# A gated block with attention and a Hadamard feed-forward: gate and up as features by tokens, the norm from squares, a new order

## The chip, the cores and the metric

The kernel runs on one core of a Trainium2 chip. The metric is device time in microseconds, the median of several executions. TensorE is called PE here, its weight loads PEld, VectorE DVE, ScalarE ACT, GpSimd POOL, and the queue that issues most transfers SP.

## What is computed

Sixteen batches of 128 tokens and 512 features go through attention on a given context and then through a feed-forward whose activations are rotated by a Walsh-Hadamard transform and rounded to 8 bits, and whose weights are rounded to -1, 0 or 1.

```python
x = x + tanh(g_xattn[0]) * xattn(layernorm(x), ctx, ctx)      # 32 query heads, 8 key heads, width 16
x = x + tanh(g_ffn[0]) * ffn(layernorm(x), w_gate, w_up, w_down)

def h_bitlinear(x, w):
    return einsum('bsh,oh->bso', act_quant(fwht(x)), weight_quant(w))
def act_quant(x):      # per token
    scale = 127.0 / clip(max(abs(x), axis=-1), EPS)
    return clip(round(x * scale), -128, 127) / scale
def weight_quant(w):
    scale = clip(mean(abs(w)), EPS)
    return clip(round(w / scale), -1, 1) * scale
def ffn(h, w_gate, w_up, w_down):          # 512 -> 2048 -> 512
    gate, up = h_bitlinear(h, w_gate), h_bitlinear(h, w_up)
    return h_bitlinear(silu(gate) * up, w_down)
```

## The kernel before

The kernel is cut into small step functions, one for each batch `b` and part. A step may `yield`, and each mention of it in the text `ORDER` (line 23) runs it on to its next `yield`; a token such as `gate.9.1` stands for `gate(9, 1)`. The order of the tokens is the program order, and the class `InOrder` keeps every engine to it, so that all instructions have the line of that helper (249) in the profile. Each engine works strictly through its own list, and waits where an operand is not ready. There is no loop and no scheduler beside that text: it alone interleaves the batches.

A batch passes through these steps:

- Attention: `moments_q` (line 390; mean and variance on DVE, three small POOL operations), `normed` (ACT), `q_transposed`, `scores` (PE, with maxima `mx` on DVE out of PSUM), `split_max` (four small POOL operations), a transpose of the maxima, `weights` (PE tiles `sT`, exponentials `ex` on ACT), `summed` (PE tiles `av`), `residual` (line 522; PE transposes `tpo`, DVE `rden` and `ga`, POOL adds into `x`).
- Into the feed-forward: `moments_h` (line 635) and `in_norm` (line 638): a second layer norm, `hn` on ACT, then two butterfly stages on POOL (tiles `hn`, `hb`); `in_turned` and `in_hadamard` (PE, tile `z`); `in_scale` (line 672), the largest magnitude on DVE and from it the scale `ae`, its inverse `re` and, on POOL, the two factors `dq` with which gate and up are to be scaled back; `in_quant` (line 682), rounding on ACT into `qe`, a transposing transfer by SP into `qTe`, and a conversion.
- `gate` and `up` (lines 708 and 714), in two halves `m` of 1024 features each. `product` (line 696) holds the 128 tokens as the stationary operand and streams 512 columns of weights: the result has tokens on partitions. ACT makes Silu of the gate with the token's factor `dq` as its scale, into `sg`; DVE multiplies up by its factor and by `sg`, into `h`.
- `hidden_transposed` (line 723): four PE transposes (`tpf`) for each 512 features and a copy `hT`, as the Hadamard transform wants features on partitions. `hadamard`, `hadamard_l` and `hadamard_p` (PE, tile `y`, a 128-point transform; the last two take one butterfly stage with it) and a copy into `za` or `zb`; `butterfly` on DVE; `magnitudes` on ACT.
- `out_scale`, `out_quant` (line 816 on; DVE, then a transposing transfer into `qTf`), `out_down` (line 872; PE tile `yo`, then on DVE the last scaling and the addition of `x`, tile `res`, which SP writes out).

Weights are loaded, summed up (`mag`), averaged (`mean`), rounded (`whole`) and clipped while the first batches are in attention. `warm` are matmuls without use ahead of the first work, `table` loads an activation table (0: the one with exponentials, 1: with Silu); the build adds a load wherever an activation finds the wrong table. `copies[k]` (line 358) is ACT for `k` = 0 and DVE for 1; `k` is the last number of many tokens. PSUM has two pools: `ps_s`, two buffers of two banks, for scores, weights, gate and up, and `ps_x`, four of one bank, for the rest.

Of the kernel before, what the change touches and what calls it, by code (L numbers as in the profile page):

```python
# [23 lines left out]
load_kv0 load_aux warm.0.12 load_x1 load_g.1 fetch.2 moments_q.0 load_g.0 load_g.3 table.0.0  # L24
gates_in load_sel moments_q.0 normed.0 q_transposed.0 load_g.2 q_transposed.0 mag_g.1 scores.0.1
fetch.4 load_u.2 moments_q.1 moments_q.1 warm.1.6 scores.0.1 scores.0.1 normed.1 moments_q.2
scores.0.0 moments_q.2 load_u.3 q_transposed.1 scores.0.0 warm.2.8 q_transposed.1 values_in.1
mag_g.0 scores.0.0 values_in.0 moments_q.3 load_u.1 scores.1.1 mag_g.3 moments_q.3 warm.3.4
scores.1.1 load_u.0 warm.4.2 scores.1.1 split_max.0 max_transposed.0.1 normed.2 max_transposed.0.1
scores.1.0 sel_in mag_g.2 q_transposed.2 scores.1.0 scores.1.0 warm.5.6 mean_g q_transposed.2  # L30
normed.3 weights.0.1 mean_g whole_g.3 whole_g.1 warm.6.8 weights.0.1 weights.0.1 whole_g.0 load_d.0
load_d.3 weights.0.0 moments_q.5 moments_q.5 summed.0.1 mag_u.3.1 weights.0.0 load_d.2 weights.0.0
split_max.1 mag_u.2 scores.2.1 clipped_g.0 max_transposed.1 scores.2.1 summed.0.0.1 max_transposed.1
summed.0.1 residual.0.1 scores.2.1 whole_g.2.1 summed.0.0.1 weights.1.0 residual.0.1 moments_q.4
q_transposed.3.1 weights.1.0 residual.0.0 q_transposed.3.1 weights.1.0 residual.0.0 residual.0.0
mag_u.0 scores.2.0 moments_q.4 summed.1.0 residual.0.1 summed.1.0 scores.2.0 scores.2.0 mag_u.1
residual.1.0 split_max.2 weights.1.1 moments_h.0 clipped_g.3 residual.1.0 moments_h.0
max_transposed.2.1 weights.1.1 fetch.6 mean_u warm.7.8 max_transposed.2.1 mean_u weights.1.1
load_d.1 whole_u.1 in_norm.0 scores.3.1 normed.4 in_norm.0 scores.3.1 whole_u.0.1 q_transposed.4
summed.1.1 in_norm.0 scores.3.1 q_transposed.4 whole_u.3 residual.1.0 normed.5 scores.3.0  # L40
in_turned.0 scores.3.0 in_turned.0 values_in.3 whole_u.2.1 scores.3.0 in_hadamard.0 in_scale.0
split_max.3 weights.2.1 summed.1.1 clipped_u.3 residual.1.1 moments_q.6 moments_q.6 weights.2.1
weights.2.1 max_transposed.3.1 q_transposed.5.1 clipped_g.2 residual.1.1 in_quant.0 weights.2.0
in_quant.0 max_transposed.3.1 moments_q.7 residual.1.1 mag_d.0.1 weights.2.0 values_in.2 summed.2.1
weights.2.0 moments_h.1 moments_h.1 normed.6 weights.3.1 summed.2.1 q_transposed.5.1 clipped_u.1
residual.2.1 weights.3.1 clipped_u.2 q_transposed.6.1 summed.2.0 weights.3.1 residual.2.1 in_quant.0
clipped_g.1 weights.3.0 in_norm.1 mag_d.2.1 summed.2.0 in_norm.1 summed.3.1 fetch.8 weights.3.0
residual.2.0 weights.3.0 in_scale.0 gate.0.0 residual.2.0 residual.2.0 clipped_u.0 mag_d.1.1 up.0.0
table.1.1 gate.0.0 in_norm.1 summed.3.1 mag_d.3 gate.0.1 residual.2.1 q_transposed.6.1 moments_q.7
up.0.0 in_turned.1.1 hidden_transposed.0.1 in_turned.1.1 mean_d up.0.1 moments_h.2  # L50
hidden_transposed.0.1 mean_d moments_h.2 in_hadamard.1 gate.0.1 up.0.1 values_in.4 summed.3.0
values_in.5 summed.3.0 in_scale.1 scores.4.0 moments_q.8 in_scale.1 in_norm.2 hidden_transposed.0.3
scores.4.0 in_quant.1 in_norm.2 hadamard.0.1 residual.3.0 hidden_transposed.0.3 in_quant.1
scores.4.0 hadamard.0.1 hadamard.0.3 moments_q.8 whole_d.0.1 residual.3.0 scores.5.1 residual.3.1
in_norm.2 hadamard.0.3 hidden_transposed.0.2.1 scores.5.1 in_quant.1 in_turned.2 whole_d.3.1
hidden_transposed.0.0 residual.3.1 gate.1.1 scores.5.1 residual.3.0 residual.3.1
hidden_transposed.0.0 moments_q.9 in_turned.2 up.1.1 gate.1.1 moments_h.3 hidden_transposed.0.2.1
normed.7 moments_h.3 in_hadamard.2 up.1.1 hadamard.0.2.1 in_scale.2 scores.4.1 in_quant.2.1
in_scale.2 moments_q.9 hidden_transposed.1.3 in_quant.2.1 hadamard.0.0 in_norm.3 in_norm.3
scores.4.1 scores.4.1 gate.1.0 hadamard.0.0 whole_d.1.1 hadamard.0.2.1 split_max.4 butterfly.0.1  # L60
up.1.0 gate.1.0 in_quant.2.1 in_norm.3 max_turned.4 hidden_transposed.1.2 whole_d.2.1 up.1.0
gate.2.0 clipped_d.1 hidden_transposed.1.2 up.2.0 hidden_transposed.1.3 gate.2.0 butterfly.0.1
butterfly.0.2 hidden_transposed.1.0 hadamard.1.2 up.2.0 hadamard.1.3.1 hidden_transposed.1.0
butterfly.0.2 butterfly.0.4 hadamard.1.2 weights.4.0 in_turned.3 table.2.0 weights.4.0
hidden_transposed.2.0.1 hadamard.1.3.1 hadamard.1.0.1 butterfly.0.4 weights.4.0
hidden_transposed.1.1 in_turned.3 hidden_transposed.2.0.1 weights.4.1 magnitudes.0 clipped_d.3
hadamard.1.0.1 summed.4.0 clipped_d.0 weights.4.1 weights.4.1 in_hadamard.3 out_scale.0
hidden_transposed.1.1 gate.2.1 out_quant.0.1 out_scale.0 hadamard.2.0.1 in_scale.3 out_quant.0.1
table.3.1 gate.2.1 summed.4.1 hadamard.2.0.1 in_scale.3 summed.4.0 scores.5.0 out_quant.0.0.1
values_in.6 in_quant.3 summed.4.1 in_quant.3 residual.4.0 scores.5.0 hadamard.1.1 out_quant.0.0.1  # L70
residual.4.1 residual.4.0 up.2.1 scores.5.0 residual.4.0 in_quant.3 residual.4.1 split_max.5
gate.3.0 up.2.1 hadamard.1.1 out_quant.0.1 butterfly.1.1 butterfly.1.1 residual.4.1 max_turned.5
hidden_transposed.2.1 up.3.0 hidden_transposed.2.1 gate.3.0 out_quant.0.0.1 hadamard.2.1 up.3.0
hidden_transposed.2.3 hadamard.2.1 butterfly.1.2 hidden_transposed.3.0 hidden_transposed.2.3
weights.5.1 butterfly.1.2 hadamard.2.3 table.4.0 weights.5.1 butterfly.1.4 hidden_transposed.3.1
weights.5.1 q_transposed.7 hadamard.2.3 scores.6.0 hidden_transposed.3.0 moments_h.4
hidden_transposed.3.1 summed.5.1 butterfly.1.4 magnitudes.1 scores.6.0 hidden_transposed.2.2
scores.6.0 hadamard.3.0.1 moments_h.4 in_norm.4 out_scale.1 scores.6.1 q_transposed.7 summed.5.1
hadamard.3.1 out_scale.1 in_norm.4 residual.5.1 hadamard.3.1 scores.6.1 scores.6.1 gate.3.1
# [181 lines left out]
def flamingo_kernel(  # L261
# [71 lines left out]
    ones = const.tile([P, P], F32, name="ones")  # L333
    nc.vector.memset(ones, 1.0)
    mhalf = const.tile([P, 1], F32, name="mhalf")
    nc.vector.memset(mhalf, -0.5)
    tanh_g = const.tile([P, 2], F32, name="tanh_g")


# [656 lines left out]
```

## Time and profile before

| what | value |
|---|---|
| median of 3 runs | 458.73 us (458.08 to 459.64) |
| the profiled execution's span | 456.3 us, 8222 instructions |
| granted TensorE clock | 1.000 |
| HBM | read 20.12 MB, written 4.19 MB |
| chain that ended last, by engine | PE 74%, DVE 10%, DMA 6%, POOL 3%, ACT 3%, issue 2% |

The span is from the first to the last instruction of one profiled execution; the runs' times are a little longer, as what lies around it is counted in. The profile gives busy time by engine, the same in 40 slices of the span, groups of equal instructions with busy time, mean duration and the idle time ahead of them, and the chain of work that ended last, followed back from the end. A matmul's duration is its latency: in a row of matmuls they overlap, and one starts well before the last has ended.

### The profile page before, as it was taken

To read this page: it belongs to the slowest core of one execution; us is meant where nothing else is said; L and a number is where in the kernel's file an instruction comes from. 1 tells how busy PE (TensorE), PEld (TensorE's weight loads), DVE (VectorE), ACT (ScalarE), POOL (GpSimd) and SP (SyncE) were. 2 spreads that over 40 slices of the span, in tenths; PEclk is the share of its full clock that TensorE was granted. 3 is DMA by queue.
4 is the path that set the end of the run, shared out by engine and by line. 5 is a ranking of instruction groups with operands and counts; after the bars stand their busy time and mean duration, and the time that the engine had idled before them with its cause. 6 is when DMAs were issued, how large, how long until landed. Compare 5 with 4: busy or idle time off the path is not lost.

```text
span 456.3 us, 8222 instructions
## 1 busy us (share of the span) xinstructions
PE 441.8 (97%) x3191; PEld 266.2 (58%) x3228; DVE 416.8 (91%) x624; ACT 324.2 (71%) x391; POOL 174.8 (38%) x316
## 2 busy tenths in 40 slices
PE   7999899999999999999999999999999999999996
PEld 3534447665665465666555665565556656576862
DVE  4898998999999999999999899989789999989995
ACT  4779897788787677596977878575776748645641
POOL 3315656512241713237274632358152542251000
PEclk9999999999999999999999999999999999999999
DMA  8998220003011153051131513030023503111331
GB/s 283 404 410 272 90 82 13 13 12 59 13 31 29 36 139 83 13 153 33 36 57 36 139 23 70 2 88 18 1 57 47 71 0 62 45 23 37 69 70 69
DMA packets 59350, 36.38 MB, mean 80 GB/s; under 512 B 47792, under 2 KB 52144, under 8 KB 58288
## 3 DMA queue, kind: packets, MB, share of 16 engines
q1 hardware_dynamic: 59312, 35.86, 29.2%
q8 instruction: 25, 0.41, 0.4%
q14 instruction: 13, 0.11, 0.1%
HBM read 20.12 MB, written 4.19 MB: 53 GB/s over the span
## 4 chain that ended last, share of the span: by engine, by line
PE 74%; DVE 10%; DMA 6%; POOL 3%; ACT 3%; issue 2%; SPq 1%; DVEq 0%; POOLq 0%; ACTq 0%
PE y L249 13%; PE yo L249 11%; PE up L249 10%; PE gate L249 10%; PE sT L249 7%; PE tpf L249 6%; PE sc L249 6%; PE av L249 6%; DMA wq_down<-in_w_up 3%; DVE mx L249 3%; PE z L249 3%; PE tpo L249 2%; DVE zb L249 2%; DMA wst_gate<-in_w_gate 2%; DVE h L249 1%
## 5 line engine op out<-in xcount | busy, mean ns | idle before, releaser
L249 DVE TENSOR_REDUCE mx<-sc 128x8 f32<-128x1024 f32 x64 | 75.5, 1217 | 8.6 <-PE sc L249 8.3
L249 PEld LDWEIGHTS <-qTe 128*128 128x128 bf16 x512 | 50.0, 98 | 52.9 <-DVE mx L249 0.8
L249 DVE TENSOR_TENSOR zb<-za 128x1024 f32<-128x1024 f32 (+1 forms) x62 | 72.7, 1198 | 1.4 <-ACT za L249 0.7
L249 PE MATMUL y<-aux,hT 128*128 128x128 f32 x544 | 72.5, 278 | 0.3 <-ACT za L249 0.2
L249 PEld LDWEIGHTS y<-aux,hT 128*128 128x128 f32 x544 | 66.7, 192 | 9.8 <-issue 3.5
L249 ACT ACTIVATE ex<-sT 128x1024 f32<-128x1024 f32 x64 | 62.7, 1026 | 12.1 <-PE sT L249 11.7
L249 PE MATMUL up<-wq_up,qTe 128*128 128x512 bf16 x247 | 60.0, 379 | 0.5
L249 PE MATMUL gate<-wq_gate,qTe 128*128 128x512 bf16 x239 | 59.6, 379 | 0.9
L249 PE MATMUL yo<-wq_down,qTf 128*128 128x512 bf16 x245 | 58.7, 379 | 0.6
L249 POOL TENSOR_TENSOR x<-x,ga 128x256 f32<-128x256 f32 x32 | 30.1, 946 | 47.7 <-DVE ga L249 47.5
L249 DVE SCALAR_TENSOR_TENSOR h<-up,dq,sg 128x1024 f32<-128x1024 f32 x32 | 41.0, 1281 | 7.7 <-ACT sg L249 4.7
L249 ACT ACTIVATE sg<-gate,dq 128x1024 f32<-128x1024 f32 x32 | 35.7, 1116 | 15.5 <-PE gate L249 12.4
L249 PE MATMUL sc<-kb,qT 32*128 32x256 f32 x512 | 40.5, 402 | 1.6 <-ACT qT L249 0.7
L249 PEld LDWEIGHTS <-qTf 128*128 128x128 bf16 x256 | 24.4, 98 | 29.1 <-issue 1.3
L249 PE MATMUL sT<-qT,kb 32*128 32x512 f32 x256 | 40.8, 640 | 0.5 <-DVE h L249 0.2
L249 DVE TENSOR_TENSOR za<-zb 128x1024 f32<-128x1024 f32 (+1 forms) x38 | 39.3, 1059 | 0.2
L249 DVE CUSTOM_DVE_ANT_0 qf<-zb,rf 128x1024 int16<-128x1024 f32 (+1 forms) x32 | 38.9, 1224 | 0.2
L249 ACT COPY hT<-tpf 128x512 f32<-128x512 f32 x45 | 26.1, 591 | 18.2 <-PE tpf L249 16.5
L249 PE MATMUL tpf<-ident,h 128*128 128x128 f32 x256 | 38.0, 277 | 0.4 <-DVE h L249 0.2
L249 PEld LDWEIGHTS tpf<-ident,h 128*128 128x128 f32 x256 | 29.0, 141 | 14.2 <-issue 6.9
L249 POOL TENSOR_TENSOR hb<-hn 128x256 f32<-128x256 f32 x32 | 25.8, 828 | 28.4 <-ACT hn L249 18.1
L249 PEld LDWEIGHTS sc<-kb,qT 32*128 32x128 f32 x512 | 25.1, 184 | 17.8 <-issue 6.5
(128 smaller groups left out, 728.1 us busy)
## 6 DMA issues: line engine op xcount, KB each, us to landing
wst_gate<-in_w_gate SPq DMA_DIRECT2D x4, 1024.0 KB, 9.6
wst_down<-in_w_down SPq DMA_DIRECT2D x4, 1024.0 KB, 12.7
out<-res SPq DMA_DIRECT2D x16, 256.0 KB, 2.2
x<-in_x SPq DMA_DIRECT2D x7, 512.0 KB, 4.1
kb<-in_kb SPq DMA_DIRECT2D x8, 256.0 KB, 4.1
wq_down<-in_w_up SPq DMA_DIRECT2D x2, 1024.0 KB, 14.1
wst_up<-in_w_up SPq DMA_DIRECT2D x2, 1024.0 KB, 15.2
kv<-in_kv SPq DMA_DIRECT2D x8, 128.0 KB, 3.9
```

The lines of the kernel that those rows point to most:

```text
L249: ins = f(*args, **kwargs)
```

## The change

Six things are changed.

1. `product` holds a 128x128 block of weights and streams the 128 tokens: the result has features on partitions, eight blocks to a PSUM tile. 2048 matmuls 128 wide with a weight load each take the place of 512 that were 512 wide. `hidden_transposed`, its transposes and copies go; the transforms read `h` as it is.
2. A token's factor now lies along the free dimension. A new step `spread` brings the gate's factor onto all partitions by a matmul with the identity and a copy (`row`, `rowb`). `gate` multiplies by it on DVE, and ACT makes Silu in place; `up` is multiplied by that and left without its factor, which the last scaling takes up.
3. The second layer norm goes. The butterflies read `x`; the mean falls out by a Hadamard matrix whose first column is zero (`had_mid`), and a new step `in_power` sums the squares of the transform on ACT, from which POOL makes the norm's factor, `dq`, and the floor of the later scale.
4. In `out_down` of batches 0 to 13, ACT scales and POOL adds `x`; 14 and 15 stay as they were.
5. Several steps are cut finer by more `yield`s.
6. `ORDER` is new throughout, and with it which copies are ACT's or DVE's; its 26 `table` tokens stand elsewhere. Over the whole program there are 48 table loads, for 26 before.

```diff
+    had_mid = const.tile([P, P], F32, name="had_mid")
-    wsc = const.tile([P, 3], F32, name="wsc")
+    wsc = const.tile([P, 5], F32, name="wsc")
...
     def absmax_scale(...):
+        yield
         a = tiny.tile([P, 1], F32, tag="a" + name, name=f"a{name}_{b}")
-        nc.vector.tensor_scalar(a, amax, 1.0 / 127.0, EPS / norm / 127.0, ALU.mult, ALU.max)
+        nc.vector.tensor_scalar(a, amax, 1.0 / 127.0, floor if name == "e" else floor(), ALU.mult, ALU.max)
+        levels[name, b] = a
+        yield
...
-    def moments_h(b: int):
-        return moments(b, "f")
     def in_norm(b: int):
-        hn = w1.tile([P, KC, P], F32, tag="hn", name=f"hn_{b}")
-        layer_norm(b, "f", hn.rearrange("p c f -> p (c f)"), xs[b])
-        src = hn
+        src = xs[b].rearrange("p (c f) -> p c f", c=KC)
...
     def in_hadamard(b: int):
...
-            nc.tensor.matmul(z[:, c, :], lhsT=hbT[:, c, :], rhs=had, start=True, stop=True)
+            nc.tensor.matmul(
+                z[:, c, :], lhsT=hbT[:, c, :], rhs=had if c else had_mid, start=True, stop=True
+            )
...
+    def in_power(b: int):
+        z = zes[b].rearrange("p c f -> p (c f)")
+        ins[b] = w1.tile([P, E], I16, tag="qe", name=f"qe_{b}")
+        power = tiny.tile([P, 1], F32, tag="power", name=f"power_{b}")
+        nc.scalar.activation(ins[b].bitcast(BF16), z, AF.Square, accum_out=power)
+        yield
+        ve = tiny.tile([P, 1], F32, tag="ve", name=f"vef_{b}")
+        nc.gpsimd.tensor_scalar(ve, power, 1.0 / E**2, EPS, ALU.mult, ALU.add)
+        yield
+        rstd = tiny.tile([P, 1], F32, tag="rstd", name=f"rstdf_{b}")
+        nc.gpsimd.tensor_tensor(rstd, ve, mhalf, ALU.pow)
+        yield
+        a = levels["e", b]
         dq = tiny.tile([P, 2], F32, tag="dq", name=f"dq_{b}")
-        nc.gpsimd.tensor_scalar(dq, wsc[:, 0:2], a, 1.0, ALU.mult, ALU.mult)
+        nc.gpsimd.tensor_scalar(dq, wsc[:, 0:2], a, rstd, ALU.mult, ALU.mult)
         dqs[b] = dq
+        yield
+        root = tiny.tile([P, 1], F32, tag="nm", name=f"root_{b}")
+        nc.gpsimd.tensor_tensor(root, ve, half, ALU.pow)
+        yield
+        floor = tiny.tile([P, 1], F32, tag="floor", name=f"floor_{b}")
+        nc.gpsimd.tensor_scalar(floor, root, rs["e", b], wsc[:, 3:4], ALU.mult, ALU.mult)
+        floors[b] = floor
+
+    def spread(b: int, k: int = 0):
+        row = ps_x.tile([P, P], F32, tag="x", name=f"row_{b}")
+        nc.tensor.matmul(
+            row, lhsT=dqs[b][:, 0:1].to_broadcast([P, P]), rhs=ident, start=True, stop=True
+        )
+        yield
+        rows[b] = w2.tile([P, P], F32, tag="row", name=f"rowb_{b}")
+        copies[k](rows[b], row)
...
     def product(b: int, m: int, w: str):
-        gu = ps_s.tile([P, 2, 512], F32, tag="s", name=f"{w}_{b}_{m}")
-        for j in range(2):
+        gu = ps_s.tile([P, 8, P], F32, tag="s", name=f"{w}_{b}_{m}")
+        for j in range(8):
             for c in range(KC):
                 nc.tensor.matmul(
-                    gu[:, j, :], lhsT=ins[b][:, c, :],
-                    rhs=wq[w][c][:, (2 * m + j) * 512 : (2 * m + j + 1) * 512],
+                    gu[:, j, :],
+                    lhsT=wq[w][c][:, (8 * m + j) * P : (8 * m + j + 1) * P],
+                    rhs=ins[b][:, c, :],
                     start=(c == 0), stop=(c == KC - 1),
                 )
         return gu
     def gate(b: int, m: int):
         gu = product(b, m, "gate")
         yield
-        sgs[b, m] = w1.tile([P, 2, 512], F32, tag="sg", name=f"sg_{b}_{m}")
-        nc.scalar.activation(sgs[b, m], gu, AF.Silu, scale=dqs[b][:, 0:1])
+        sg = w3.tile([P, 8, P], F32, tag="sg", name=f"sg_{b}_{m}")
+        nc.vector.tensor_tensor(sg, gu, rows[b].unsqueeze(1).to_broadcast([P, 8, P]), ALU.mult)
+        yield
+        nc.scalar.activation(sg, sg, AF.Silu)
+        sgs[b, m] = sg
     def up(b: int, m: int):
         gu = product(b, m, "up")
         yield
-        h = w2.tile([P, 2, 512], F32, tag="h", name=f"h_{b}_{m}")
-        nc.vector.scalar_tensor_tensor(
-            h, gu, dqs[b][:, 1:2], sgs.pop((b, m)), ALU.mult, ALU.mult
-        )
+        h = sgs.pop((b, m))
+        nc.vector.tensor_tensor(h, gu, h, ALU.mult)
         hs[b, m] = h
-    def hidden_transposed(b: int, n: int, k: int = 0):
...
+    def turned(b: int, n: int):
+        return hs[b, n // 2][:, 4 * (n % 2) : 4 * (n % 2) + 4, :]
...
     def out_down(b: int, k: int, parts: int = 2):
...
-            nc.vector.scalar_tensor_tensor(res, y, scs[b], xs[b], ALU.mult, ALU.add)
+            if b < 14:
+                nc.scalar.activation(res, y, AF.Copy, scale=scs[b])
+                yield
+                nc.gpsimd.tensor_tensor(res, res, xs[b], ALU.add)
+            else:
+                nc.vector.scalar_tensor_tensor(res, y, scs[b], xs[b], ALU.mult, ALU.add)
```

A piece of the two orders, from the middle:

```diff
-scores.9.0 scores.9.0 in_quant.6 hadamard.5.3.1 in_norm.7 gate.6.0 table.11.1 gate.6.0 in_norm.7
-residual.8.1 up.6.0 moments_q.10 out_down.2.1 gate.6.1 hadamard.5.3.1 butterfly.5.1 up.6.0
...
+values_in.11 gate.9.0 up.9.0 moments_q.13 normed.13 spread.9 out_down.5.1 q_transposed.13
+summed.11.0 summed.11.1 gate.9.0 out_quant.7.0 out_quant.7.0 gate.9.0 up.9.0 out_quant.7.0
...
```

## The prediction

> **What bounds the kernel now.** I read the busy shares first, then the slices, then a table of stretches, then the groups, and last the chain of waits and the timeline for the pace of single matmuls. The page's engine and slice lines:
>
> ```profile
> PE 441.8 (97%) x3191; PEld 266.2 (58%) x3228; DVE 416.8 (91%) x624; ACT 324.2 (71%) x391; POOL 174.8 (38%) x316
> PE   7999899999999999999999999999999999999996
> DVE  4898998999999999999999899989789999989995
> PEclk9999999999999999999999999999999999999999
> ```
>
> PE has work nearly all the time at the full granted clock, and DVE is only six points behind. Three stretches (us; then busy time of PE, PEld, DVE, ACT, POOL, with the count of instructions) show where each is short of work:
>
> ```profile
> 0.00:10.00 10.00, 6.71 (x35) 3.10 (x36) 3.42 (x8) 3.69 (x5) 4.35 (x18) 1.00 0.82 264
> 230.00:260.00 30.00, 29.84 (x214) 17.80 (x216) 27.56 (x39) 23.59 (x30) 19.62 (x21) 1.00 0.31 71
> 450.00:456.30 6.30, 2.54 (x14) 1.10 (x13) 1.39 (x4) 0.29 (x1) 0.00 (x0) 1.00 0.13 47
> ```
>
> Over twenty such stretches PE idles 14.5 us: 7.6 before 60 us (loads), 3.7 after 450, and only 3.2 in the 390 us between. There PE sets the pace. DVE idles 39.5 us: 15.8 at the two ends and 23.7 in the middle. Of its waits, those for PE come to some 16 us (8.3 of them the maxima waiting for scores) and those for ACT to 7. So PE is first, DVE a close second: a microsecond taken from PE counts until DVE's own 416.8 + 15.8 = 432.6 is reached.
>
> **The rows that give the prices** (busy us, mean ns of one):
>
> ```profile
> L249 PE MATMUL tpf<-ident,h 128*128 128x128 f32 x256 | 38.0, 277 | 0.4 <-DVE h L249 0.2
> L249 DVE SCALAR_TENSOR_TENSOR h<-up,dq,sg 128x1024 f32<-128x1024 f32 x32 | 41.0, 1281 | 7.7 <-ACT sg L249 4.7 <-PE up L249 2.6
> L249 DVE TENSOR_TENSOR zb<-za 128x1024 f32<-128x1024 f32 x58 | 70.1, 1233 | 1.3 <-ACT za L249 0.7
> L249 DVE BATCH_NORM_STATS2 stf<-x 128x6 f32<-128x512 f32 x16 | 10.9, 681 | 0.2 <-POOL x L249 0.2
> L249 DVE COPY hT<-tpf 128x512 f32<-128x512 f32 x19 | 12.7, 679 | 0.2 <-issue 0.2
> L249 DVE COPY za<-y 128x512 f32<-128x512 f32 x22 | 14.9, 681 | 1.5 <-PE y L249 1.5
> L249 ACT COPY hT<-tpf 128x512 f32<-128x512 f32 x45 | 26.1, 591 | 18.2 <-PE tpf L249 16.5 <-PE y L249 1.4 <-ACT ex L249 0.3
> L249 ACT ACT_TABLE_LOAD x26 | 33.4, 1283 | 1.2 <-PEq L984 0.7
> L249 ACT ACTIVATE qe<-z,re 128x512 int16<-128x512 f32 x16 | 11.1, 693 | 8.9 <-DVE re L249 6.4 <-issue 1.4 <-PE sc L249 1.1
> L249 POOL TENSOR_TENSOR hn<-hb 128x256 f32<-128x256 f32 x32 | 26.5, 850 | 0.9
> ```
>
> A matmul's mean is its latency, not its cost in a row of them. The cost is in the chain of work (start, us, piece) and, for a bf16 matmul 128 wide, in the timeline of the last transposes, each with its own weight load:
>
> ```profile
> 426.51 0.44 PE tpf L249 x4
> 429.11 3.57 PE y L249 x32
> ```
>
> ```profile
> 281.38 1.73 PE up L249 x8
> ```
>
> ```profile
> 447.26 0.28 PEld L249 LDWEIGHTS <-qf 128*128 128x128 bf16 x4 [0.26 <-DVE unused L249]
> 447.33 0.39 PE L249 MATMUL tpf_q<-ident,qf 128*128 128x128 bf16 x4
> ```
>
> The reader sees 0.216 us for a 512-wide gate or up matmul (1.73 / 8), 0.110 for a transpose (0.44 / 4), 0.112 for one of the two passes of a 128-wide f32 matmul (3.57 / 32). Four bf16 pairs of load and matmul take 0.39 us, and one alone lasts 0.219 (the median of its tile's view), so each further pair costs (0.39 - 0.219) / 3 = 0.057 us. The load's 98 ns therefore hide behind the matmul before it.
>
> **PE, part by part.** The instruction lists of the two kernels give the counts.
> - Gate and up, tokens as rows: 512 x 0.216 = 110.6 us go. As features by tokens: 2048 pairs x 0.057 = 116.7 us come. Net +6.1. Upper bound: if the load did not hide, its 0.098 would be the pace, 200.7 us, +90.1. Lower bound: 0.054, a quarter of the 512-wide matmul, 0. I take 0.057, for it is the very pair of operations; a burst of four is short, and I keep the upper end for a rival.
> - The 256 transposes of the hidden values go: 256 x 0.110 = 28.2 by the chain, 38.0 by busy time (their 64 groups' fill and drain with it).
> - Spreading the scale over partitions (`spread`) adds 16 f32 matmuls of two passes, 32 x 0.112 = +3.6.
> - Sum: 6.1 - 28.2 + 3.6 = -18.5; with the busy figure -28.3. I take -18.5, since PE ran back to back and the fill of a group lies under the next.
>
> One rule speaks against this. The Trainium skill, "TensorE: Matmul & The Clock Gate", Back-to-back issue gap, says that a sustained stream of weight load and matmul at 128 columns costs about 81 ns each. By it the products would take 2048 x 0.081 = 166 us and the sum would be +31, not -18.5. The timeline row of this case says 57 ns; no long stream of such pairs is in this trace.
>
> **DVE.** Goes: second layer norm's moments, 16 x (0.681 + 0.182) = 13.8; `hT` copies 12.7; 14 of 22 `za` copies moved to ACT, 9.5; 14 of 16 last scalings `res` at 0.740, 10.4; weight magnitudes and rounding moved to ACT, net 5.8; `qTf` and others, about 0. Comes: the gate's scaling by the spread row, 32 tensor by tensor products of 128x1024 out of PSUM. None like it is in the trace; the nearest are the butterfly (1.233) and the same size out of PSUM with a scalar (1.281): 38.9 to 41.0, and I take 1.233, 39.5, as it is the same operation. The up product turns from the scalar form to that one, 32 x 0.048 = -1.5. Row copies and rest +1. Sum: 416.8 - 13.8 - 12.7 - 9.5 - 10.4 - 5.8 + 39.5 - 1.5 + 1 = 403.6. With the ends' 15.8 idle its floor is 419.4.
>
> **ACT.** Goes: `hT` 26.1, `hn` 13.1. Comes: the squares with their sum, nearest `qe` 0.693 plus an accumulator read of 0.19, 16 x 0.88 = 14.1; `res` 14 x 0.69 = 9.7; `za` 14 x 0.59 = 8.3; row copies 13 x 0.31 = 4; weight steps 6; others 0. The table tokens keep their number, but the order puts many where they do not serve, and the build holds 48 table loads for 26: 22 x 1.283 = 28.2. Sum: 324.2 - 39.2 + 14.1 + 9.7 + 8.3 + 4 + 6 + 28.2 = 355, or 81% of a 437 us span. The cover is ACT's idle time: PE or DVE would end last all the same.
>
> Here too a rule is dearer than the row. The Trainium skill, "ScalarE: Activation LUTs", What ACT_TABLE_LOAD costs, adds a drain of about 1.38 us to each switch, 30 us more for these 22, and ACT at 385. The row shows 1.2 us idle in all ahead of 26 loads, so the drain does not show here.
>
> **POOL** gets the last addition, 14 x 1.7 (twice `hn`'s 0.850; from 1.1, by the slope from 0.715 at 128 columns, to 1.9, twice the residual's 0.946), 23.8, and small steps `root` and `floor`, 16 x (0.57 + 0.45) = 16.3, less `nm` 6.4: 208.5, under half. Queued behind the addition are the next batch's butterflies and split maxima; SP's output transfer follows it, 14 times far from the end. The last two batches keep DVE's scaling, so the end keeps its length.
>
> **SP and the start.** SP issues the same 115 transfers in a new order: one part of down's weights now stands ahead of up's, and batches 8 and 9 ahead of the last three parts of down; no load is added. Before 60 us PE idles 7.6 us; the new order can win these or lose as much again by starving a stage, and I take 0, as the bytes are the same.
>
> **The new wait.** The gate now goes DVE, ACT, DVE: scaling, Silu in place, product with up. While Silu runs, DVE has what the order puts between. Summed at the prices above, less 0.06 us that neighbours overlap, this covers Silu (1.05) and a load just ahead of it (1.283) in 24 of 32 cases; the other 8 lack 9.7 us in all, or 2.3 if the loads, which wait for no data, run early. DVE's floor becomes 419.4 + 2.3 to 9.7 = 422 to 429, still under PE.
>
> **Sum.** PE: 456.3 - 18.5 = 437.8 us of span, above DVE's 422 to 429. The median lies 2.4 us above the profiled span (458.73 - 456.3): 437.8 + 2.4 = 440.2, so 440.
>
> **Rivals.**
> - DVE becomes the bound and keeps its middle idle: 403.6 + 39.5 + 2.4 = 445.5, and with the 9.7 on top 455. For: both engines are now within 5% of each other, so each waits for the other more. Against: most of its idle time was waiting for PE, which is faster.
> - More than the chain's price is won: -28.3, and PE's 3.2 idle in the middle: 456.3 - 31.5 + 2.4 = 427. For: finer steps. Against: PE was already at 99% there.
> - Slower, by the table loads: the 22 added loads land in the chain scaling, Silu, product, and DVE and then PE wait out each: 440.2 + 28.2 = 468. It decides from (458.7 - 440.2) / 1.283, 15 loads in the path. For: ACT at 81% is behind more often and runs strictly in its order, with exponentials behind Silu. Against: the cover counted above.
> - The products do not run as fast as four pairs do: each ns over 57 costs 2.05 us, slower from 66 ns, 524 at 98 ns. For: weight loads now alternate with every short matmul for 3.6 us on end. Against: the second to fourth pairs keep an even 57 ns.
>
> **How the numbers follow.** No change is anything within 0.3%, 1.4 us, about what a measurement of this kernel can tell. Chances: forecast (430 to 449) 0.53; DVE bound (449 to 457) 0.13; more won (under 430) 0.09; nothing measurable 0.03; table loads (over 460) 0.13; product pace 0.09. Faster 0.75, same 0.03, slower 0.22. The range runs from 427, the second price in full, to 463, into the table loads' case; beyond lie some 0.05 below and 0.15 above.
>
> **What would show it.** Right: gate and up pieces of 32 pairs near 1.83 us in the chain; PE busy near 423 and still at 97%; DVE near 404; 48 table loads and ACT near 355; no `tpf`, no `hT`. Wrong: pieces over 2.1 us (pace); `sg` or its product on DVE with over 15 us idle before them, released by ACT (loads); idle time on PE in the middle well over 3 us (DVE or ACT has become the bound); PE short of work by much more than 7.6 us before 60 us (loads).

## The result, and the profile after

The changed kernel takes 473.86 us (median of 4 runs, 472.95 to 475.48), the kernel before, beside it, 458.46 us. The ratio is 1.033 (95% interval 1.030 to 1.036): slower by 15.4 us, where 18.5 us less had been forecast.

The profiled execution of the changed kernel has a span of 473.7 us. Its page, busy time by engine and then four of the rows by slice:

```profile
PE 443.9 (94%) x4520; PEld 314.4 (66%) x4540; DVE 415.0 (88%) x580; ACT 351.1 (74%) x429; POOL 232.1 (49%) x349
...
PE   7897999998999899999899999999998999999986
...
DVE  4797778998898999799898997998989797999985
ACT  4997788699789566688859869784887859776452
...
PEclk9996899999999999999999999999999999999999
```

PE was to be busy for some 423 us and is for 443.9; it idles 29.8 us, where before it idled 14.5. The extra 15.3 us of idle time and 2.1 us of busy time are the whole difference of the spans (17.4). In the 390 us from 60 to 450 it idles 14.6 us, where before it idled 3.2: a sign that the prediction named for being wrong. DVE, at 88%, is not busier than before either.

The groups show that most prices were right (busy us, mean ns of one, then the idle time ahead of them and its releasers):

```profile
L255 ACT ACT_TABLE_LOAD x48 | 61.6, 1283 | 1.5 <-PEq L1039 0.7
L255 DVE TENSOR_TENSOR sg<-gate,rowb 128x1024 f32<-128x1024 f32 x32 | 39.0, 1219 | 5.7 <-PE gate L255 4.6 <-ACT rowb L255 0.6 <-issue 0.2
L255 DVE TENSOR_TENSOR sg<-up,sg 128x1024 f32<-128x1024 f32 x32 | 38.9, 1218 | 9.5 <-ACT sg L255 7.7 <-ACT za L255 1.2 <-PE up L255 0.5
L255 ACT ACTIVATE sg<-sg 128x1024 f32<-128x1024 f32 x32 | 33.4, 1055 | 13.4 <-DVE sg L255 13.3
L255 ACT ACTIVATE qe<-z 128x512 bf16<-128x512 f32 x16 | 9.6, 598 | 11.3 <-DVE amax_e L255 9.5 <-issue 1.5
L255 DVE TENSOR_TENSOR zb<-za 128x1024 f32<-128x1024 f32 x58 | 73.4, 1290 | 3.7 <-ACT za L255 3.0 <-DVE za L255 0.5
L255 DVE CUSTOM_DVE_ANT_0 qf<-zb,rf 128x1024 int16<-128x1024 f32 x28 | 38.2, 1380 | 0.4
```

The last two rows are work that the change does not touch, and it has become dearer: the butterfly from 1233 to 1290 ns, the rounding `qf` from 1293 to 1380. The rows above show waits at the places where an engine hands a tile to another and takes it back.

The chain of waits, first its shares by engine from the page:

```profile
PE 42%; DVE 25%; ACT 18%; DMA 6%; issue 5%; SPq 2%; POOL 1%; ACTq 0%; DVEq 0%; POOLq 0%
```

and some of its pieces (start, us, what):

```profile
68.58 3.57 PE gate L255 x64
...
251.49 1.28 ACT L255
252.78 1.06 ACT sg L255
253.85 1.28 ACT L255
```

PE's share of the chain fell from 74% to 42%. The first piece is 64 pairs of weight load and matmul in 3.57 us, 0.056 each: the pace that the forecast took. The last pieces are ACT alone, with table loads (the lines named only `ACT L255`, of 1.28 us) on both sides of a Silu.

PE's time can be split by the start times of its matmuls alone, which need no modelled end: its work (each matmul at the normal spacing of its kind, records that the trace lacks included), the gaps in and between its groups, and the rest at the two ends.

| kernel | PE's work | gaps | ends | span |
|---|---|---|---|---|
| before | 404.0 | 45.8 | 6.5 | 456.3 |
| changed | 383.8 | 84.8 | 5.1 | 473.7 |

So 20.2 us of work left PE, as priced (18.5), and 39.0 us of gaps came. Work is counted at the spacing of the full clock, so what matmuls lose at half clock is among the gaps: with 17.1 us at half clock in this execution, at most 8.5 us of them.

### The profile page after: what moved, and what is told of

It is laid out like the page before. It is cut to its first block, busy times and chain, and to the rows that moved or that the text cites. A ratio compares the mean times of both kernels' runs of the same rounds, so it can differ in the third digit from the quotient of the medians.

```text
span 473.7 us, 10926 instructions
## 1 busy us (share of the span) xinstructions
PE 443.9 (94%) x4520; PEld 314.4 (66%) x4540; DVE 415.0 (88%) x580; ACT 351.1 (74%) x429; POOL 232.1 (49%) x349
## 4 chain that ended last, share of the span: by engine, by line
PE 42%; DVE 25%; ACT 18%; DMA 6%; issue 5%; SPq 2%; POOL 1%; ACTq 0%; DVEq 0%; POOLq 0%
PE sT L255 6%; PE gate L255 6%; PE y L255 5%; DVE qf L255 5%; PE sc L255 5%; DVE mx L255 5%; PE up L255 5%; DVE zb L255 5%; ACT L255 5%; PE yo L255 4%; PE av L255 4%; DVE sg L255 3%; ACT ex L255 3%; DVE za L255 3%; ACT za L255 3%
## 5 line engine op out<-in xcount | busy, mean ns | idle before, releaser
L255 DVE TENSOR_REDUCE mx<-sc 128x8 f32<-128x1024 f32 x64 | 75.3, 1218 | 11.3 <-PE sc L255 10.0
L255 DVE TENSOR_TENSOR zb<-za 128x1024 f32<-128x1024 f32 (+1 forms) x62 | 76.0, 1251 | 3.8 <-ACT za L255 3.0
L255 PE MATMUL y<-aux,sg 128*128 128x128 f32 x544 | 73.3, 281 | 1.6 <-DVE sg L255 1.1
L255 PEld LDWEIGHTS y<-aux,sg 128*128 128x128 f32 x544 | 65.3, 192 | 14.0 <-issue 6.1
L255 ACT ACTIVATE ex<-sT 128x1024 f32<-128x1024 f32 x64 | 62.4, 1024 | 11.2 <-PE sT L255 10.9
L255 PE MATMUL gate<-qTe,wq_gate 128*128 128x128 bf16 x1024 | 61.3, 219 | 2.6 <-DVE mx L255 1.1
L255 PEld LDWEIGHTS <-wq_gate 128*128 128x128 bf16 x1024 | 59.0, 98 | 5.4 <-issue 4.6
L255 PE MATMUL up<-qTe,wq_up 128*128 128x128 bf16 x1024 | 61.4, 219 | 1.1 <-ACT ex L255 1.0
L255 PEld LDWEIGHTS <-wq_up 128*128 128x128 bf16 x1024 | 58.9, 98 | 1.8 <-issue 1.4
L255 PE MATMUL yo<-wq_down,qTf 128*128 128x512 bf16 x236 | 56.8, 379 | 2.8 <-DVE qTf L255 1.3
L255 PE MATMUL sc<-kb,qT 32*128 32x256 f32 x512 | 46.0, 418 | 8.0 <-ACT ex L255 3.3
L255 POOL TENSOR_TENSOR x<-x,ga 128x256 f32<-128x256 f32 x32 | 27.2, 861 | 42.5 <-DVE ga L255 41.1
L255 PE MATMUL sT<-qT,kb 32*128 32x512 f32 x256 | 46.4, 655 | 1.4 <-DVE mx L255 0.5
L255 DVE TENSOR_TENSOR sg<-up,sg 128x1024 f32<-128x1024 f32 x32 | 38.9, 1218 | 9.5 <-ACT sg L255 7.7
L255 PEld LDWEIGHTS sc<-kb,qT 32*128 32x128 f32 x512 | 28.1, 191 | 25.6 <-ACT ex L255 9.5
L255 PEld LDWEIGHTS <-qTf 128*128 128x128 bf16 x256 | 23.7, 98 | 30.7 <-issue 3.6
L255 DVE TENSOR_TENSOR sg<-gate,rowb 128x1024 f32<-128x1024 f32 x32 | 39.0, 1219 | 5.7 <-PE gate L255 4.6
L255 ACT ACTIVATE sg<-sg 128x1024 f32<-128x1024 f32 x32 | 33.4, 1055 | 13.4 <-DVE sg L255 13.3
L255 POOL TENSOR_TENSOR res<-res,x 128x512 f32<-128x512 f32 x14 | 22.5, 1612 | 41.2 <-ACT res L255 41.1
L255 DVE CUSTOM_DVE_ANT_0 qf<-zb,rf 128x1024 int16<-128x1024 f32 (+1 forms) x32 | 42.0, 1329 | 0.5
L255 DVE TENSOR_TENSOR za<-zb 128x1024 f32<-128x1024 f32 (+1 forms) x38 | 39.7, 1077 | 0.2
```

What stands on the lines that cost most here:

```text
L255: ins = f(*args, **kwargs)
```

## The experiments

The times are medians in us; the ratio is to the kernel before on the same chip, with its 95% interval.

| run | what it is | time | ratio |
|---|---|---|---|
| e1 | changed, without the 26 `table` tokens | 468.85 | 1.022 (1.021 to 1.024) |
| e2 | changed, two `warm` tokens moved | 475.55 | 1.038 (1.035 to 1.040) |
| e3 | e1 and e2 | 469.1 | 1.022 (1.018 to 1.027) |
| e4 | changed steps in before's order | 515.83 | 1.124 (1.122 to 1.126) |
| e5 | before, with only the last scaling moved | 462.74 | 1.009 (1.008 to 1.011) |
| e6 | before, with only the norm from squares | 472.08 | 1.029 (1.027 to 1.031) |
| e7 | before, with only the new products | 495.86 | 1.082 (1.079 to 1.086) |
| e8 | e1, last scaling on DVE again | 472.93 | 1.031 (1.027 to 1.035) |
| e9 | e1's steps, new order | 467.27 | 1.019 (1.017 to 1.022) |
| e10 | before without table tokens, new order | 478.83 | 1.045 (1.043 to 1.047) |
| e11 | e8's steps, new order | 467.2 | 1.019 (1.016 to 1.021) |
| e12 | changed, new order, waits of e9 and e10 counted | 459.69 | 1.001 (1.000 to 1.003) |
| e13 | before, new order in the same way | 460.78 | 1.004 (1.002 to 1.005) |
| e14 | as e12, clock counted too | 461.6 | 1.006 (1.004 to 1.008) |
| e15 | as e13, clock counted too | 459.81 | 1.003 (1.002 to 1.004) |
| e16 | e12 with 17 us less work on DVE | 456.28 | 0.994 (0.992 to 0.996) |
| e17 | e12 with 14 us less work on PE | 457.36 | 0.997 (0.994 to 0.999) |
| e18 | before with 14 us less work on PE | 453.64 | 0.990 (0.986 to 0.993) |

### Table loads and the clock (e1, e2, e3)

```diff
-table.24.0 moments_q.0 table.10.0 load_aux warm.0.12 warm.4.2
+moments_q.0 load_aux warm.0.12 warm.4.2
```

e1 takes all 26 such tokens away; the build then adds the loads that are needed, 26 in place of 48.

> The changed kernel without the 26 table tokens in the order; the build alone places loads, 26 instead of 48. Theory T (table loads stand in the path): the chain of the changed kernel holds some 17 loads, 22 us; with 22 loads fewer the time falls by 12 to 25 us, to 449-462. Rival W (waits of the new order between the engines, whatever ACT is loaded with): ACT has slack, the loads gone only lengthen ACT's waits, at most 4 us, 470-474. Rival C (halved granted clock at 38-52 us costs most): no change, 472-475.

It took 468.85 us, 5.0 less than the changed kernel. In the chain the loads held some 22 us; taking 22 loads of 1.283 away won less than a quarter of that. The next wait was never far behind.

In e2 two `warm` tokens stand earlier, as in the changed kernel the granted clock is halved for 13.65 us from 38.3 us on, and for 3.4 us later:

```diff
-residual.0.1 scores.2.0
+residual.0.1 warm.6.8 scores.2.0
...
-split_max.2 weights.1.1
+split_max.2 warm.3.4 weights.1.1
...
-out_scale.1 warm.6.8 gate.3.1
+out_scale.1 gate.3.1
...
-in_norm.7 warm.3.4 hadamard.5.1
+in_norm.7 hadamard.5.1
```

> The changed kernel with two of its idle matmul groups (8 and 4) moved from later stages to the two places between 35 and 41 us where PE ran dry. Theory C: the granted clock stays at 1.00 between 35 and 60 us, that stretch gets 5 to 7 us shorter, time 466-469. Theory T and W: the stretch is bound by ACT and DVE there as much as by PE, gain 0 to 3, 471-474.

The clock rose from 0.982 to 0.996 in the profiled execution (0.982 to 0.996 over the four), the time did not fall (475.55). e3 has both edits:

> Both edits together. If T and C are separate costs the gains add: 442-457. If they overlap (the clock fell because ACT's loads starved PE), the time is that of the kernel without table tokens.

469.1, e1's time. That does not make the halved clock free. The executions of one kernel differ in how much of them runs at half clock, and those with more of it take longer: e3 took 470.8 and 470.9 us at a mean clock of 0.985, but 466.8 and 467.4 at 0.993 and 1.000; e12 below, in twelve executions, took 457.7 at 0.993 and 460.5 to 460.9 at 0.985. At a like clock the moved `warm` costs some 2 us (e3's 470.8 against 468.9 of e1, both at 0.985), and the higher clock gives them back. How much of the 15.4 us goes with the clock was not measured by itself; as an estimate, at the slopes of e1 (0.8 us for 0.007) and e12 (3.0 us for 0.008) the changed kernel's 0.982 stands for 2 to 7 us. The order decides where PE runs short, so this is a part of the order's price.

### The parts one by one (e4 to e8)

e4 keeps the changed arithmetic and puts its tokens where the order before had them, copies on the engines that they had there, as in this piece, against the order before:

```diff
-gate.9.0 out_quant.7.1 hadamard.8.3 out_quant.7.0 out_quant.7.0 hadamard.8.2 butterfly.8.1 out_down.6.1 up.9.0 table.17.1 gate.9.0
+gate.9.0 spread.9 out_quant.7.1 hadamard.8.3 out_quant.7.0 out_quant.7.0 hadamard.8.2 butterfly.8.1 out_down.6.1 up.9.0 table.17.1 spread.9 gate.9.0 gate.9.0
```

> All arithmetic of the changed kernel, but in the order of the kernel before: its tokens, with those for steps that are gone left out and those for the finer or new steps set beside the step they belong to; table tokens as before, 26 loads. Theory O (the new order is what costs, the arithmetic saves what was priced): faster than before, 438-452. Theory A (the arithmetic costs: more hand-overs between DVE, ACT and POOL for each batch than the PE time that it saves): slower than before, 462-480, with PE idle in the middle well over 3 us.

515.83: in that order it is worse by far, 56.8 us behind before. e7 shows most of why, with the products alone, in before's order and on before's kernel:

```diff
-gate.0.0 residual.2.0 residual.2.0 clipped_u.0 mag_d.1.1 up.0.0 table.1.1 gate.0.0
+gate.0.0 spread.0 residual.2.0 residual.2.0 clipped_u.0 mag_d.1.1 up.0.0 table.1.1 spread.0 gate.0.0 gate.0.0
```

> The kernel before, its order, with gate and up as features by tokens, without transposes, as the only edit. By the prices PE loses 18.5 us, ACT 26, and DVE gains 39.5 - 12.7 - 1.5 = 25.3 to 442 busy, which with 15.8 idle at the ends is 458. Theory D (DVE becomes the bound, nothing else is lost): 458-470, DVE at 94% or more. Theory H (the hand-over scaling, Silu, product stalls both DVE and ACT): 480-515, DVE at 88% or less, with over 40 us of ACT waiting for DVE ahead of Silu.

It took 37 us more than before. The groups of e7:

```profile
L223 DVE TENSOR_TENSOR sg<-up,sg 128x1024 f32<-128x1024 f32 x32 | 39.1, 1221 | 12.2 <-ACT sg L223 8.8 <-PE up L223 3.3
L223 DVE TENSOR_TENSOR sg<-gate,rowb 128x1024 f32<-128x1024 f32 x32 | 39.0, 1218 | 10.2 <-ACT rowb L223 10.1
L223 ACT ACTIVATE sg<-sg 128x1024 f32<-128x1024 f32 x32 | 33.8, 1057 | 75.6 <-DVE sg L223 75.6
```

Before, ACT made Silu straight from PE's result. Now DVE must scale first, and where DVE stands in its list when the gate is ready decides how long ACT stands still: 75.6 us in 32 waits, with everything queued behind Silu on ACT. The operations themselves cost what was forecast (1218 and 1221 ns), and DVE was busy for 440.1 us. The new hand-over is what costs, until an order is made for it; the changed order cuts this wait to 13.3 us.

e6, the norm alone, with `in_power` in place of `moments_h`:

```diff
-        layer_norm(b, "f", hn.rearrange("p c f -> p (c f)"), xs[b])
-        src = hn
+        src = xs[b].rearrange("p (c f) -> p c f", c=KC)
...
+        nc.scalar.activation(ins[b].bitcast(BF16), z, AF.Square, accum_out=power)
```

> The kernel before, its order, with the second norm from the transform's squares as the only edit (16 moments and 16 normalisations fewer, 16 squares on ACT and 48 small POOL steps in their place). Theory O: PE sets the pace, 455-460. Theory A: the squares stand between the transform and the rounding on ACT, and the longer POOL chain delays the gate's Silu; 461-470.

13.6 us more than before. Two of its waits (us in total, times, longest):

```profile
DVE mx L251 <- PE sc L251: 17.8, 18, 5.4
ACT qe L251 <- DVE amax_e L251: 14.8, 9, 4.8
```

The second is new and was not in the forecast: the magnitude on DVE and the squares on ACT only read the same transform `z` in PSUM, and yet the one waits for the other, and what ACT has behind it waits too. In e9, whose order has them the other way round, DVE waits for ACT. Its timeline, ACT first:

```profile
69.75 0.60 ACT L253 ACTIVATE qe<-z 128x512 bf16<-128x512 f32 x1
```

and DVE:

```profile
70.48 0.69 DVE L253 TENSOR_REDUCE amax_e<-z 128x1 f32<-128x512 f32 x1 [2.61 <-ACT qe L253]
```

Whichever stands second in the program waits. The changed kernel pays 9.5 us of such waits on ACT.

e5, the last scaling alone:

```diff
-            nc.vector.scalar_tensor_tensor(res, y, scs[b], xs[b], ALU.mult, ALU.add)
+            if b < 14:
+                nc.scalar.activation(res, y, AF.Copy, scale=scs[b])
+                yield
+                nc.gpsimd.tensor_tensor(res, res, xs[b], ALU.add)
```

> The kernel before, its order, with the last scaling of batches 0 to 13 on ACT and POOL as the only edit. DVE loses 10.4 us, ACT gains 9.7, POOL some 23. Theory A (hand-overs and POOL's work cost): POOL's additions slow DVE beside them, the butterfly's mean rises from 1.233 to 1.26 us or more, time 461-468. Theory O (this arithmetic is sound): PE sets the pace as before, 456-460.

4.2 us more than before, though DVE had lost 10.4 us of work. Its busy time stayed at 416.2 us, and the groups say why:

```profile
L250 DVE TENSOR_TENSOR zb<-za 128x1024 f32<-128x1024 f32 x58 | 73.3, 1290 | 0.7
L250 DVE CUSTOM_DVE_ANT_0 qf<-zb,rf 128x1024 int16<-128x1024 f32 x28 | 38.7, 1388 | 0.2
```

Nearly the same means as in the changed kernel (1290 and 1380), and all that was added beside DVE are 14 scalings on ACT and 14 additions on GpSimd (1442 ns each). DVE's product out of PSUM did not change (1280 ns for 1281). The trace tells the two engines apart. Of the 58 butterflies of this row, 30 have no instruction of GpSimd beside them and take 1219 ns on average, and 1221 ns where ACT is busy over four fifths of that time (21 of them); the 28 with one beside them take 1365. In the kernel before, 37 without take 1220. The longest stands beside one of the new additions. GpSimd's timeline in e5:

```profile
143.03 1.65 POOL L250 TENSOR_TENSOR res<-res,x 128x512 f32<-128x512 f32 x1 [8.63 <-ACT res L250]
```

and DVE's, two butterflies, of which the second takes 2.30 us:

```profile
142.32 3.45 DVE L250 TENSOR_TENSOR zb<-za 128x1024 f32<-128x1024 f32 x2
```

The same two in the kernel before:

```profile
141.82 2.35 DVE L249 TENSOR_TENSOR zb<-za 128x1024 f32<-128x1024 f32 x2
```

So it is GpSimd's work, not ACT's, that lengthens DVE's operations on SBUF, and only some of those that it meets.

e8 puts this one part back in e1:

```diff
-            if b < 14:
-                nc.scalar.activation(res, y, AF.Copy, scale=scs[b])
-                yield
-                nc.gpsimd.tensor_tensor(res, res, xs[b], ALU.add)
-            else:
-                nc.vector.scalar_tensor_tensor(res, y, scs[b], xs[b], ALU.mult, ALU.add)
+            nc.vector.scalar_tensor_tensor(res, y, scs[b], xs[b], ALU.mult, ALU.add)
```

> The changed kernel without table tokens, with the last scaling of all batches back on DVE in one instruction. Contention theory: with 22 us less of POOL's additions the butterfly's mean falls from 1.29 to 1.25 us, which pays for the 10.4 us on DVE; 463-470. Theory W (waits between engines in the new order): DVE's added work delays its other products, 470-478, with butterflies as slow as before.

472.93, 4.1 slower than e1: in the changed order the moved scaling does help a little. (`qf` fell back to 1306 ns, the butterfly stayed at 1289: in this order it is mostly GpSimd's own butterflies, `hn`, that stand beside those of DVE, and those of DVE without an instruction of GpSimd beside them take 1217 ns here too.) In the order of before the three parts alone lose 37.4, 13.6 and 4.2 us, 55.2 of the 56.8 that e4 loses with all of them. Each part loses in an order that was not made for it, and what a part is worth cannot be read from it alone.

### New orders (e9 to e15)

Here the tokens were moved one at a time, with the durations of the traces added up along each engine's list, for both arithmetics alike. The same place in the order of the changed kernel and of e9, and in that of before and of e10; e11 is e8's steps treated likewise:

```diff
-weights.11.1 q_transposed.12 values_in.11 gate.9.0 up.9.0 moments_q.13 normed.13 spread.9
+in_quant.9.1 weights.11.1 residual.10.0 gate.9.0 hadamard.8.0 butterfly.7.2 moments_q.13
...
-hadamard.8.3 weights.11.1 weights.11.1 gate.9.0 out_quant.7.1 hadamard.8.3 out_quant.7.0
+in_scale.9 summed.11.0 weights.11.1 gate.9.0 up.9.0 out_down.4.1 q_transposed.12
```

> All arithmetic of the changed kernel, without table tokens, in another order: the tokens were moved one at a time wherever that shortened the program worked out from the durations in the traces of the two kernels. Theory O (the arithmetic saves about what was priced, the changed kernel's order gives it back in waits): 428-450, PE and DVE each at 93% or more. Theory A (the arithmetic cannot be ordered so that it gains: more hand-overs, DVE slowed by POOL): 458-475, with waits of DVE for ACT and PE as before.

> The kernel before, without table tokens, reordered in the same way and with the same effort. It tells how much of a gain of the reordered changed kernel is the order's alone. Theory O: the order before was near its best, 445-458, and the reordered changed kernel is at least 8 us faster than this one. Theory A: at or below the reordered changed kernel.

> The changed kernel with the last scaling of all batches on DVE, without table tokens, reordered in the same way. If POOL's additions slow DVE by as much as they relieve it (contention), this is within 3 us of the reordered changed kernel; if the move to ACT and POOL is worth its price, this is 5 to 10 us slower.

467.27, 478.83 and 467.2: in equally searched orders the changed arithmetic was 11.6 us ahead, and where the last scaling is made was worth nothing; but all were slower than before. The traces showed what these orders had not counted. One is in the groups of e10:

```profile
L245 ACT ACT_TABLE_LOAD x26 | 33.4, 1283 | 18.6 <-PE gate L245 13.4 <-DMA x<-in_x 3.6 <-issue 1.3
```

A table load that the build adds stood still until PE's gate was done, 13.4 us in all, so it could no longer be hidden in ACT's idle time; a `table` token, ahead of it, can (1.2 us before 26 loads in the kernel before). The others are the two readers of `z` and PE's gaps at a change of kind (last section). e12 and e13 count these and keep their tokens. The same place in e12 and e14 against the changed kernel, then in e13 and e15 against before:

```diff
-weights.11.1 q_transposed.12 values_in.11 gate.9.0 up.9.0 moments_q.13 normed.13 spread.9
+spread.9 residual.10.1 out_down.5.1 gate.9.0 fetch.14 butterfly.7.4 butterfly.7.4 hadamard.8.3
+spread.9 weights.11.1 in_norm.10 gate.9.0 in_norm.10 up.9.0 out_down.3.1 butterfly.7.2
...
-hadamard.8.3 weights.11.1 weights.11.1 gate.9.0 out_quant.7.1 hadamard.8.3 out_quant.7.0
+hadamard.8.0.1 in_scale.9 normed.13 gate.9.0 weights.11.0 up.9.0 weights.11.0
+hadamard.8.0.1 weights.11.1 moments_h.10 gate.9.0 butterfly.7.2 weights.11.1 butterfly.7.2
```

> The changed kernel's own steps and its 26 table tokens, only in another order: tokens moved one at a time by the durations that the earlier runs' traces show, now with three costs counted that the order of e9 left out: a table load that the build adds ahead of an activation on a PSUM tile waits for that tile (13.4 us of ACT's idle time lie ahead of such loads in e10); the two readers of one transform z, the largest magnitude on DVE and the squares on ACT, do not overlap (e9: magnitude 2.61 us late, released by the squares); and PE loses 0.25 to 0.42 us whenever it leaves scores, weights or sums for something else. Theory A (the changed arithmetic is cheaper and only its order loses): at most 455 us, near 447, ratio to before under 0.992. Theory B (what was moved onto ACT and GpSimd slows DVE and the hand-overs so much that no order makes up for it): 462 us or more, near e9's 467.

> The arithmetic and the 26 table tokens of before, its order searched in the same way and for as long as that of e12. Theory A: by the same sums it ends some 8 to 12 us behind e12, at 452 to 460, so that the difference of e12 to before comes from the change and not from the search alone. Theory B: it ends level with e12 or ahead of it.

e12, with the very steps of the changed kernel, took 459.69 us, 14.2 less than it, and cannot be told from before. It beat e13 by 1.1 us. Neither theory's number came: 455 was not reached, and 462 was beaten. Its page and its chain:

```profile
PE 437.8 (96%) x4540; PEld 313.0 (68%) x4540; DVE 414.9 (91%) x580; ACT 337.0 (74%) x420; POOL 256.8 (56%) x349
...
PE 62%; DVE 22%; ACT 6%; POOL 3%; issue 3%; DMA 3%; SPq 1%; DVEq 0%; ACTq 0%; POOLq 0%
```

> As e12, the changed kernel with its tokens in another order, with one more cost counted: the granted clock. In e12 it was halved twice in the first 35 us, each time after a stretch of 3.4 us in which PE was busy for under three quarters, and by 35 us e12 lay some 7 us behind its own sums, where before lay on them. Here the order also keeps PE fed and the eight warm tokens spread where it would else fall short. Theory A (the changed arithmetic wins once its waits are placed): 450 to 456 us, ratio under 0.995. Theory B (DVE, some 92% busy with work that the additions on GpSimd lengthen, holds it level with before): 457 to 461, ratio 0.997 to 1.005.

> The arithmetic of before with its order searched once more in the same way and for as long as that of e14. Theory A: 455 to 460 us, behind e14 by at least 2 us. Theory B: within 2 us of e14.

461.6 and 459.81: now the old arithmetic is ahead by 1.8 us. The clock was not kept in e14: its executions had 0.981 (465.0 us) to 0.996 (458.9 us), e12's 0.985 to 0.993, while e13 and e15 had 0.993 to 1.000. Part of what the changed arithmetic lacks thus goes with its clock, and how it would stand at the full one is open. So with orders of like quality the two arithmetics are level within some 2 us, and no order that was tried beats the 458.5 of before.

### What a microsecond of PE or DVE is worth (e16, e17, e18)

```diff
-        nc.vector.tensor_tensor(h, gu, h, ALU.mult)
+        nc.vector.tensor_tensor(h[:, :4], gu[:, :4], h[:, :4], ALU.mult)
```

> The kernel of e12 with less work on DVE: the product of up and the gate covers the first 512 of 1024 columns, so that half of the hidden values are the gate's Silu alone. By the rows of e12 (1.215 us at 1024 columns, 0.69 at 512) DVE loses 32 x 0.53 = 17 us of 415. Theory A (with the changed arithmetic DVE sets the pace, so what PE was spared does not arrive): the time falls by 9 to 17 us from e12's 459.7, to 443 to 451. Theory B (PE still sets it): it falls by under 4 us.

e17 and e18 shorten the sums of `up`, in e12 and in the kernel before:

```diff
+        nc_ = 3 if w == "up" else KC
...
-            for c in range(KC):
+            for c in range(nc_):
```

> The kernel of e12 with less work on PE: up's products sum three of the four blocks of features, so 256 pairs fall away, 256 x 0.056 = 14.3 us of PE. Theory A: the time falls by under 4 us from e12's 459.7. Theory B: it falls by 9 to 14 us, to 446 to 451.

> The kernel before, its own order, with the same cut: up's products sum three of the four blocks, 64 matmuls of 512 columns fewer, 64 x 0.216 = 13.8 us of PE. The prediction's premise (PE sets the pace of before, and what is taken from it arrives until DVE's 432.6 is reached): it falls by 11 to 14 us, to 445 to 448. Rival (PE and DVE bind by turns, so that a saving on PE alone is mostly lost in waiting for DVE): it falls by under 6 us.

None of the three gave what its engine was spared: e16 3.4 us of 17 (456.28 against 459.69), e17 2.3 of 14.3, e18 5.2 of 13.8 (by the interval of its ratio 3.2 to 6.2). The split of PE's time says where the rest went:

| kernel | PE's work | gaps | ends | span |
|---|---|---|---|---|
| e12 | 383.8 | 67.7 | 6.5 | 458.0 |
| e17, PE cut | 369.5 | 80.9 | 6.1 | 456.5 |
| before | 404.0 | 45.8 | 6.5 | 456.3 |
| e18, PE cut | 390.2 | 57.3 | 6.5 | 454.0 |

The work that was cut came back as gaps, 13.2 of 14.3 us and 11.5 of 13.8 by the profiled executions. That of e18 was its slowest, with one step of 3.4 us at half clock; by the medians 8.6 of its 13.8 us did not arrive. In e17 a lower clock goes with a part of it as well: one of its ten executions had 0.995 and took 453.9 us, the others 0.984 to 0.989 and 456.3 or more. PE, spared work, came sooner to a wait: its groups of narrow matmuls (32 of 128 rows or columns: `sc`, `sT`, `av`), its changes between these and full ones and the ends stayed nearly the same, and the gaps grew between full matmuls (in e18 from 3.3 to 8.0 us between those of different tiles), with PE idle for GpSimd's `hn` and DVE's `h` for 1.7 us each, where it was under 0.5 before. And where DVE was spared, it waited: in e16 its wait for scores grew from 10.8 to 16.0 us.

## Why the prediction was wrong, step by step

- **Products at 0.057 us a pair: right.** 64 pairs took 3.57 us. The Trainium skill's figure of about 81 ns for a sustained pair at 128 columns ("TensorE: Matmul & The Clock Gate", Back-to-back issue gap) is not what this trace shows over 64 pairs on end: 56.
- **PE's sum of -18.5: right as work.** By start times it is -20.2.
- **"There PE sets the pace": this is the step that failed.** A busy share of 97% and 3.2 us of idle time in the middle were read as if each microsecond of PE's work were one of span, until DVE's 432.6 were reached. e18 took 13.8 us from PE in the kernel before, with nothing else changed, and 5.2 arrived. A matmul counts as busy to the end of its latency, so the 45.8 us of gaps between starts do not show as idle time, and the share could not tell how much of PE's pace was its own. By e16 to e18 neither PE alone nor DVE alone bounds such an order. The rival that DVE becomes the bound (445.5 to 455) fails in the same way: in the order of e12, e16 took 17 us from DVE and won 3.4.
- **The new order, priced only by its table loads and the cover of one hand-over.** The same steps in another order took 14.2 us less (e12). Nearly all of the loss of 15.4 lies there; what is left, e12 against before, is 0.1% (-0.0% to 0.3%). Of the 33.7 us between the forecast's 440.2 and the measured 473.9, 14.2 are thus the order, which the sum put at nothing for PE, and 19.5 are a saving that did not arrive in the better order either.
- **DVE at 404: it came to 415.0.** The gate's scaling cost 39.0 (39.5 forecast), but the butterflies and `qf` rose by 10.0 in all (58 x 0.057, 30 x 0.024, 28 x 0.087, 15 x 0.113 and six short or rare ones by 1.9), the effect that e5 shows of GpSimd's work beside DVE. It was put at nothing without a reason, and it takes back about what "14 of 16 last scalings, 10.4" was to give. In the changed kernel too the 28 of 58 butterflies without an instruction of GpSimd beside them take 1219 ns; GpSimd is busy for 232.1 us, where 208.5 had been forecast.
- **ACT near 355, 48 loads: right** (351.1). No drain shows with them either: 1.5 us idle ahead of 48, and Silu starts as a load ends (251.49 + 1.28, then 252.78). The rival of the table loads in the path (468) had the place right and the price wrong: the chain holds some 22 us of them, and taking 22 loads away gave 5.0.
- **The cover counted for Silu: about right** for DVE (7.7 us short, forecast 2.3 to 9.7), but only half the story. The 13.3 us that ACT waits for DVE's scaling, and the 9.5 us of the squares behind the magnitude, were not in the sum.
- **Start taken as 0: not settled.** PE is busy for 1.3 us less of the first 60 us than in the kernel before (51.1 against 52.4), but at a mean granted clock of 0.89 against 1.00, so it did less in that time. The clock was not in the sum; lower clocks go with longer times by e3 and e12, and e2, which raised it, paid for that with the moved `warm`.

What stays open: whether a better order exists for either arithmetic. Each one here is the best that was found, not the best there is, and the searched orders of before's arithmetic did not reach before's own 458.5 either.

## What to carry to other kernels

A busy share near 100% does not price a saving: leave out some of that engine's work, run it, and see how much arrives before building a change on it. In a program whose order is written out, judge arithmetic and order apart, by giving old and new arithmetic equally good orders; a step that goes from one engine to another and back needs an order made for it, or it blocks what is queued behind it. Work moved off DVE to GpSimd, which idles half the time, is not free for DVE.

## What the runs showed of the hardware

- PE pays for a change between full and narrow matmuls. The timeline of PE in the kernel before:

```profile
341.31 0.60 PE L249 MATMUL tpq<-ident,q 128*128 128x128 f32 x4
341.75 0.60 PE L249 MATMUL tpo<-ident,avT 128*128 128x128 f32 x4
342.19 0.60 PE L249 MATMUL tph<-ident,hn 128*128 128x128 f32 x4
342.72 1.15 PE L249 MATMUL sc<-kb,qT 32*128 32x256 f32 x16
```

Four transposes follow four others after 0.44 us, but the scores, 32 rows high, after 0.53. Over that trace the step into `sc`, `sT` or `av` costs 0.093 us (median of 64), the step out of `sc` or `sT` to a full matmul 0.250, from `av` to `sc` or a full one 0.415; between full matmuls of different tiles it is 0.000. By these medians the 128 steps into and out of narrow groups come to some 24 of the 45.8 us of gaps, and those among narrow groups to some 9 more, most of it inside what the page calls busy.
- GpSimd's work can lengthen the operation of DVE on SBUF that runs beside it: in e5 a butterfly of 128x1024 takes 1219 ns with no instruction of GpSimd beside it, 1365 on average with one, 2303 beside an addition of 1650 ns. Not every one does so: three beside a small `m_pad` step kept 1216. DVE's product out of PSUM is not lengthened (1280 and 1281 ns), and ACT beside it costs next to nothing (1221 ns).
- The granted clock was halved in steps of 3.41 us, each time after a step in which PE was busy for only part of it: 0.47 and 0.64 in the changed kernel, 0.48 and 0.73 in e12. In the kernel before no step between the first matmuls and the last 7 us fell below 0.77, and the clock stayed full. But steps of 0.63 and 0.71 in the changed kernel were not followed by a halving, so these traces give no bound.
- More of an execution at half clock goes with a longer time: e12 took 457.7 us at a mean of 0.993 and 460.5 to 460.9 at 0.985.
